# Last part of an attention-and-experts kernel: values of the gates in a PSUM bank, normalising spread over the products, and one copy moved to ScalarE

## The chip, the cores and the metric

The kernel runs on one core of a Trainium2 chip. Its engines are named as in the profile: PE (TensorE, matmuls and transposes), ACT (ScalarE), DVE (VectorE), POOL (GpSimd) and SP (SyncE, which here only issues DMAs). The metric is the device time of one execution in microseconds. Before the change three runs took 1736.75, 1737.0 and 1741.14 us; the median is 1737.0.

## The reference

The input is `x` of shape (4, 32, 128, 128). Two layers follow each other.

```python
# layer 0: each image becomes q of 128 channels x 4096 pixels (2x2 space-to-depth)
energy = einsum('bci,bcj->bij', q, q)          # 4096 x 4096 per image
energy = energy / (d[:, :, None] * d[:, None, :])   # d = sqrt(diagonal)
out = gamma * einsum('bcj,bij->bci', q, softmax(energy)) + xs

# layer 1, on the same values as 4 x 4096 tokens of 128 values
t = t + sum over heads of Q @ (K^T V)           # of _ln_t(t): a linear attention
probs = softmax(_ln_t(t) @ router_w + router_b)  # 8 experts
top_p, top_i = top_k(probs, 2);  top_p /= sum(top_p)
t = t + sum over the two of top_p * (_ln_t(t) @ expert_w[e] + expert_b[e])
```

The second layer has no softmax in its attention, so a product of a 128 x 128 matrix with every token is enough for it. The expert layer adds to each token the output of its two best experts, weighted by their normalised probabilities.

## The kernel before

Per image, the 4096 pixels are cut into 8 chunks of 512. A chunk is loaded, transposed by PE into a bank (`ptq`), copied to SBUF as `qT` (L302), squared and summed (L324, L325), raised to the power -1/2 by POOL (L164), scaled (L338), transposed again and copied as `qn`. This is `prep`; the chunk that everything waits for is the first one of image 0, in two halves (`g` = 0 and 1). Then `attend` walks over pairs of chunks: products of `qn` (L556), exponentials on ACT (L559), value products (L440), and, since the matrix of energies is symmetric, the mirrored share through transposed blocks (L369, L375). That is nearly all of the time, and PE sets it.

The second layer of an image runs while the next image's first layer does, except for the last image, where nothing is left to run beside it. There `last_parts` (L1183 and after) does it with all of the core. Its order is the order of the Python statements: from the end of the prologue on, the program is recorded in an order written out by hand, and each engine keeps it.

The tokens of an image are 32 tiles `k` of 128 tokens. In the last part each goes through these steps:

- The attention's product is added (L1217 to L1220, L1242), then mean and variance are taken (`bn_stats`, `close_stats`). Its power -1/2 is on POOL (L164), followed on POOL by `nbf` and `nbo` (L638, L640).
- `normalise` (L642) writes `xn[:, k]` on ACT, one instruction per tile (L644).
- `transpose_tokens(g)` (L862) turns four tiles by PE into one bank (`ptf`, L870); an ACT copy of 512 columns brings them back to `xn` (L866).
- `router_rows` (L806, lines L811 to L819) makes the eight logits per token on DVE, and `route` (L821, lines L830 to L853) the gates: maximum, exponential (ACT, L832), best and second-best expert, their weights. It is done for 16 tiles at once, so an instruction has 128 x (16 x 8) elements. `route(0)` covers tiles 0 to 15, `route(1)` tiles 16 to 31. The result `gate` is the tile `first`.
- `product(k, h)` (L1197) multiplies tile `k` by four experts (`h` = 0 or 1) into a bank `py` (L1198). Five banks go round for these. `scaled_sums` on DVE (L1141) adds some of the eight experts to `acc`, with `T` or `acc` in SBUF as the other input; `scaled_rows` on ACT (L1155) writes the others, scaled, to `tmp`: 6 of 8 for k below 8, 5 below 14, then 4. POOL adds them up for each two tiles (`sum_rows`, L1163 to L1167), and four DMAs store every four tiles (L1173).

A main loop over k holds the last three. Beside it runs the generator `second_half`, one step per turn: statistics of tiles 16 to 31, `router_rows`, `route(1)`, then normalising and transposing groups 4 to 7. Groups 0 and 1 are ready before the loop; groups 2 and 3 (tiles 8 to 15) are normalised and transposed just ahead of it.

Transposes take their bank from the pool `ps_t` of three, through `psum_t`; `hold` keeps count of banks that are not emptied yet.

Of the kernel before, what the change touches and what calls it, by code (L numbers as in the profile page):

```python
# [15 lines left out]
AF = mybir.ActivationFunctionType  # L16
ALU = mybir.AluOpType
AX = mybir.AxisListType
# [4 lines left out]
def kernel(  # L23
# [74 lines left out]
    def psum_t(name):  # L98
        return ps_t.tile([P, CH], F32, tag="pt", name=name)
# [182 lines left out]
    def prep(b, kc, st):  # L282

        if b == 0:
            if kc == 0:
                st["all"] = big1.tile([P, 4, 8, HW2, 2], F32, tag="T", name="xx_0")
            xx = st["all"][:, kc]
        else:
            xx = xin.tile([P, 8, HW2, 2], F32, tag="xx", name=f"xx_{b}_{kc}")
        first = b == 0 and kc == 0  # L290
        load_tokens(
            xx.rearrange("p k w r -> p k (w r)"), b, 8 * kc, 8, (nc.sync, nc.scalar if first else nc.sync)
        )
        qT = qpool.tile([P, 2, NJ, P], F32, tag="qT", name=f"qT_{b}_{kc}")
        st.setdefault("qT", {})[2 * kc] = qT[:, 0]
        st["qT"][2 * kc + 1] = qT[:, 1]
        yield
        yield
        yield from idle(2 if b else 1)

        def load_half(g, pt):
            nc.vector.tensor_copy(  # L302
                qT[:, :, 2 * g : 2 * g + 2, :].rearrange("p s j (r c) -> p (j r) s c", c=64),
                pt.rearrange("p (m s c) -> p m s c", s=2, c=64),
            )

        for g in range(2):
            yield
            pt, done = hold(f"ptq_{b}_{kc}_{g}", partial(load_half, g))
            for jj in range(2):  # L310
                for r2 in range(2):
                    k = 4 * g + 2 * jj
                    nc.tensor.transpose(
                        pt[:, ts(2 * jj + r2, P)], xx[:, k : k + 2, :, r2].rearrange("p k w -> p (k w)"), ident
                    )
            yield
            done()
        yield
        yield
        ss = stat.tile([P, 2 * NJ], F32, tag="ss", name=f"ss_{b}_{kc}")  # L320
        rn = stat.tile([P, 2 * NJ, 1], F32, tag="rn", name=f"rn_{b}_{kc}")
        for s in range(2):
            sq = work.tile([P, NJ, P], F32, tag="qs", name=f"sq_{b}_{kc}_{s}", bufs=2)
            nc.vector.tensor_tensor(sq, qT[:, s], qT[:, s], ALU.mult)  # L324
            nc.vector.tensor_reduce(ss[:, ts(s, NJ)], sq, AX.X, ALU.add)  # L325
            if first:
                pow_neg_half(rn[:, ts(s, NJ), 0], ss[:, ts(s, NJ)])
            elif s == 1:
                pow_neg_half(rn[:, :, 0], ss)
            yield  # L330
            yield
        yield from idle(1)
        if first:
            keep_running(22, ps_g, "pg")
        scaled = []
        for s in range(2):
            qs = work.tile([P, NJ, P], F32, tag="qs", name=f"qs_{b}_{kc}_{s}", bufs=2)
            nc.vector.tensor_tensor(qs, qT[:, s], rn[:, ts(s, NJ)].to_broadcast([P, NJ, P]), ALU.mult)  # L338
            scaled.append(qs)
        for s, qs in enumerate(scaled):  # L340
            yield
            qn = npool.tile([P, CH], F32, tag="qn", name=f"qn_{b}_{2 * kc + s}")
            st.setdefault("qn", {})[2 * kc + s] = qn
            pt, done = hold(f"ptn_{b}_{kc}_{s}", lambda p, qn=qn: nc.scalar.activation(qn, p, AF.Copy))  # L344
            for j in range(NJ):
                nc.tensor.transpose(pt[:, ts(j, P)], qs[:, j, :], ident)
            yield
            done()
        yield
        yield  # L350
# [251 lines left out]
    def layer1(b, st):  # L602
# [200 lines left out]
                    bank[:, ts(j - j0, D + 2 * E)], keep[k // 4][:, ts(k % 4, P)], matx, start=True, stop=True  # L803
                )

        def router_rows(eng, r0, nr, la):  # L806

            sh = [P, nr, E]
            rows = slice(r0, r0 + nr)
            w1, w2 = (stat.tile([P, 16, E], F32, tag=nm, name=f"{nm}_{b}_{r0}", bufs=1)[:, :nr] for nm in ("lw1", "lw2"))  # L810
            eng.tensor_tensor(w1, nba[:, rows].to_broadcast(sh), srw.to_broadcast(sh), ALU.mult)  # L811
            eng.tensor_tensor(w1, la[:, :, E:], w1, ALU.subtract)
            eng.tensor_tensor(w1, w1, sda[:, rows].to_broadcast(sh), ALU.mult)
            eng.tensor_tensor(w1, w1, la[:, :, :E], ALU.add)
            yield
            eng.tensor_tensor(w2, nbf[:, rows].to_broadcast(sh), srw.to_broadcast(sh), ALU.mult)
            eng.tensor_tensor(w2, w2, rb_sb.to_broadcast(sh), ALU.add)
            eng.tensor_tensor(w1, w1, rsf[:, rows].to_broadcast(sh), ALU.mult)
            eng.tensor_tensor(lg[:, rows], w1, w2, ALU.add)  # L819

        def route(h):  # L821

            sh = [P, KT // 2, E]
            rows = slice(h * KT // 2, (h + 1) * KT // 2)
            ms, dn = (stat.tile([P, KT // 2, 1], F32, tag=nm, name=f"{nm}_{b}_{h}") for nm in ("ms", "dn"))
            pr = stat.tile(sh, F32, tag="prob", name=f"prob_{b}_{h}", bufs=1)
            mx = weight[:, 1, rows]
            o1, o2 = first[:, rows], second[:, rows]
            v = lg[:, rows]
            nc.vector.tensor_reduce(mx, v, AX.X, ALU.max)  # L830
            nc.vector.tensor_tensor(pr, v, mx.to_broadcast(sh), ALU.subtract)
            nc.scalar.activation(pr, pr, AF.Exp)  # L832
            yield
            nc.vector.scalar_tensor_tensor(o1, pr, 1.0, rank.to_broadcast(sh), ALU.is_equal, ALU.mult)
            nc.vector.tensor_reduce(ms, o1, AX.X, ALU.max)
            nc.vector.tensor_tensor(o1, o1, ms.to_broadcast(sh), ALU.is_equal)
            nc.vector.scalar_tensor_tensor(pr, o1, -2.0, pr, ALU.mult, ALU.add)
            yield
            nc.vector.tensor_reduce(mx, pr, AX.X, ALU.max)
            nc.vector.tensor_tensor(o2, pr, mx.to_broadcast(sh), ALU.is_equal)  # L840
            nc.vector.tensor_tensor(o2, o2, rank.to_broadcast(sh), ALU.mult)
            nc.vector.tensor_reduce(ms, o2, AX.X, ALU.max)
            yield
            nc.vector.tensor_tensor(o2, o2, ms.to_broadcast(sh), ALU.is_equal)
            nc.vector.tensor_scalar(dn, mx, 1.0, None, ALU.add)
            nc.vector.reciprocal(dn, dn)
            if not alone:
                nc.vector.tensor_copy(weight[:, 0, rows], dn)
                nc.vector.tensor_tensor(mx, mx, dn, ALU.mult)
                return  # L850
            nc.vector.tensor_tensor(o2, o2, mx.to_broadcast(sh), ALU.mult)
            nc.vector.tensor_tensor(o1, o1, o2, ALU.add)
            nc.vector.tensor_tensor(gate[:, rows], o1, dn.to_broadcast(sh), ALU.mult)  # L853

        def add_rows(u, j0, la, pa):
            nj = min(3, 8 - j0)
# [326 lines left out]
        def last_parts():  # L1183
# [53 lines left out]
            def second_half():  # L1237

                bs, stats = batch_stats("f", 16, 16)
                for u in (2, 3):  # L1240
                    tg = T[:, ts(u, 8), :]
                    nc.vector.tensor_tensor(tg, tg, copies[u], ALU.add)  # L1242
                    yield
                    for j in range(8):
                        stats[8 * u - 16 + j]()
                        if j % 4 == 3:
                            yield
                close_stats("f", 16, 16, bs)
                yield
                logits = router_rows(nc.vector, 16, 16, la[:, 16:])  # L1250
                next(logits)
                yield
                yield
                for _ in logits:
                    pass
                gates = route(1)
                next(gates)
                yield
                for g in range(4, 8):
                    normalise(range(4 * g, 4 * g + 4), rsf, nbo)  # L1260
                    next(gates, None)
                    yield
                    transpose_tokens(g)()
                    yield
# [15 lines left out]
                pass  # L1280
            products = [product(k, h, bank(f"py_{b}_{k}_{h}")) for k in range(2) for h in range(2)]
            transpose_tokens(1)()
            normalise(range(8, 16), rsf, nbo)
            transpose_tokens(2)()
            transpose_tokens(3)()
            for k in range(KT + 4):
                if k < KT:
                    n = by_scalar(k)
# [6 lines left out]
                    sum_rows(k // 2 - 1, by_scalar(k - 2), nc.vector if k == KT else nc.gpsimd)  # L1295
                if k >= 5 and k % 4 == 1:
                    store(k // 4 - 1)
                if k >= 1:
                    next(rest, None)

# [102 lines left out]
```

## Time and profile before

| | us |
|---|---|
| median of the runs (3) | 1737.0 |
| the profiled execution | 1730.18 |
| its span, first to last instruction | 1728.4 |
| PE busy | 1656.8 (96%) |
| DVE busy | 939.3 (54%) |
| ACT busy | 925.8 (54%) |
| POOL busy | 511.8 (30%) |
| DMA, mean over the span | 206 GB/s |

All the rest is from the profiled execution, and its times count from the start of the span. The last part looks like this, by stretches (busy us of each engine):

| stretch | length | PE | DVE | ACT | POOL |
|---|---|---|---|---|---|
| 1652.0 to 1657.0 | 5.00 | 3.54 | 2.53 | 4.57 | 0.00 |
| 1657.0 to 1668.0 | 11.00 | 10.66 | 9.30 | 9.49 | 7.38 |
| 1668.0 to 1681.0 | 13.00 | 9.88 | 11.63 | 7.78 | 12.52 |
| 1681.0 to 1690.4 | 9.40 | 7.00 | 8.88 | 7.95 | 6.52 |
| 1690.4 to 1697.9 | 7.50 | 7.39 | 5.23 | 6.79 | 5.57 |
| 1697.9 to 1720.6 | 22.70 | 22.58 | 17.82 | 16.15 | 18.75 |

Where a row of the timeline merges several instructions, its duration is from the first start to the last end. "[0.16 <-PE ptq L313]" after a row is the idle time of the engine ahead of it and what ended it. [...]

### The profile page before, as it was taken

To read this page: it belongs to the slowest core of one execution; us is meant where nothing else is said; L and a number is where in the kernel's file an instruction comes from. 1 tells how busy PE (TensorE), PEld (TensorE's weight loads), DVE (VectorE), ACT (ScalarE), POOL (GpSimd) and SP (SyncE) were. 2 spreads that over 40 slices of the span, in tenths; PEclk is the share of its full clock that TensorE was granted. 3 is DMA by queue.
4 is the path that set the end of the run, shared out by engine and by line. 5 is a ranking of instruction groups with operands and counts; after the bars stand their busy time and mean duration, and the time that the engine had idled before them with its cause. 6 is when DMAs were issued, how large, how long until landed. Compare 5 with 4: busy or idle time off the path is not lost. (4 is left out here: it accounts for less than half of the span.)

```text
span 1728.4 us, 21211 instructions
## 1 busy us (share of the span) xinstructions
PE 1656.8 (96%) x5458; PEld 876.9 (51%) x5458; DVE 939.3 (54%) x2443; ACT 925.8 (54%) x2893; POOL 511.8 (30%) x553
## 2 busy tenths in 40 slices
PE   7999999999999999989999999999999999999887
PEld 4444444455554456445564455545555445544633
DVE  4433334367485235467568334557748524455686
ACT  3555445465565455446565544546656545545376
POOL 1000000011026514550014631652102650453156
PEclk9999999999999999989999999999999999999999
DMA  4775778876569899996568979998656988995001
GB/s 128 202 206 170 205 208 238 250 213 183 158 195 271 241 259 262 246 257 182 168 189 228 277 230 262 283 252 231 183 163 196 269 242 260 269 259 135 1 13 38
DMA packets 240681, 355.25 MB, mean 206 GB/s; under 512 B 27312, under 2 KB 155312, under 8 KB 226480
## 3 DMA queue, kind: packets, MB, share of 16 engines
q1 hardware_dynamic: 220048, 314.91, 64.5%
q0 software_dynamic: 12288, 25.19, 4.9%
q10 hardware_dynamic: 8224, 13.77, 2.8%
q8 instruction: 46, 0.75, 0.2%
q14 instruction: 75, 0.61, 0.1%
HBM read 183.64 MB, written 173.15 MB: 206 GB/s over the span
## 5 line engine op out<-in xcount | busy, mean ns | idle before, releaser
L559 ACT ACTIVATE pr<-pe 128x512 f32<-128x512 f32 (+1 forms) x576 | 322.4, 560 | 557.0 <-PE pe L556 428.8
L440 PE MATMUL po<-pr,qT 128*128 128x512 f32 (+3 forms) x1152 | 552.9, 562 | 3.9 <-ACT o L445 3.4
L375 PE MATMUL pg<-G,qT 128*128 128x512 f32 x880 | 453.4, 597 | 14.1 <-DMA G<-blocks 8.7
L556 PE MATMUL pe<-qn,qn 128*128 128x512 f32 x896 | 462.5, 598 | 3.3 <-ACT pr L559 3.0
L369 DVE STREAM_TRANSPOSE F<-pr 128x512 f32<-128x512 f32 x440 | 306.1, 702 | 156.1 <-ACT pr L559 132.1
L440 PEld LDWEIGHTS po<-pr,qT 128*128 128x128 f32 x1152 | 216.6, 191 | 251.8 <-issue 224.4
L380 ACT ACTIVATE junk<-G 128x512 bf16<-128x512 f32 x440 | 273.0, 621 | 7.1 <-DMA G<-blocks 7.0
L375 PEld LDWEIGHTS pg<-G,qT 128*128 128x128 f32 x880 | 167.5, 192 | 214.0 <-issue 187.0
L1114 POOL DMA_INDIRECT yb<-ys,place x192 | 185.5, 966 | 262.5 <-DMA xn<-xs 96.3
L989 POOL DMA_INDIRECT xs<-xn,place x192 | 186.1, 969 | 132.2 <-ACT pr L559 55.3
L556 PEld LDWEIGHTS pe<-qn,qn 128*128 128x128 f32 x896 | 155.3, 192 | 115.9 <-issue 103.0
L385 DVE TENSOR_TENSOR o<-o,pg 128x512 f32<-128x512 f32 x110 | 75.5, 686 | 203.1 <-PE pg L375 164.6
L164 POOL TENSOR_TENSOR rn<-ss,neg_half 128x8 f32<-128x8 f32 (+1 forms) x17 | 26.9, 1586 | 334.1 <-DVE ss L325 334.1
L559 ACT ACTIVATION_READ_ACCUMULATOR pr<-pe 128x1 f32 x576 | 112.1, 195 | 0.0
L1023 ACT ACTIVATE xn<-pys 128x256 f32<-128x256 f32 (+1 forms) x120 | 45.0, 377 | 118.3 <-PE pys L1056 67.7
L1049 PEld LDWEIGHTS pys<-ew_sb,xn 128*128 128x128 f32 x468 | 68.5, 192 | 56.3 <-issue 39.0
L164 POOL TENSOR_TENSOR rsf<-dm_f,neg_half 128x8 f32<-128x8 f32 (+1 forms) x15 | 26.2, 1748 | 233.7 <-DVE sv_f L636 233.7
L556 PE MATMUL pe<-qn 128*128 128x512 f32 (+3 forms) x256 | 91.1, 438 | 0.7 <-ACT qn L344 0.7
L164 POOL TENSOR_TENSOR rsa<-dm_a,neg_half 128x8 f32<-128x8 f32 x16 | 26.4, 1650 | 219.3 <-DVE sv_a L636 219.0
L380 ACT ACTIVATION_READ_ACCUMULATOR junk<-G 128x1 f32 x440 | 84.4, 192 | 0.0
L1049 PE MATMUL pys<-ew_sb,xn 128*128 x468 | 72.1, 277 | 11.1 <-ACT xn L1023 11.0
L1032 DVE COPY result<-pys 128x256 f32<-128x256 f32 (+1 forms) x60 | 24.6, 411 | 96.5 <-ACT xn L1023 48.7
(189 smaller groups left out, 1607.6 us busy)
## 6 DMA issues: line engine op xcount, KB each, us to landing
blocks<-F SPq DMA_DIRECT2D x108, 1024.0 KB
G<-blocks SPq DMA_DIRECT2D x432, 256.0 KB
xn<-xs SPq DMA_DIRECT2D x114, 128.0 KB
below<-F SPq DMA_DIRECT2D x31, 384.0 KB
G<-below SPq DMA_DIRECT2D x124, 96.0 KB
out_dram<-acc SPq DMA_DIRECT2D x128, 64.0 KB
xx<-in_x_dram SPq DMA_DIRECT2D x62, 128.0 KB
ys<-xn SPq DMA_DIRECT2D x60, 128.0 KB
```

The source lines that it names most:

```text
L164: pinned(nc.gpsimd.tensor_tensor(dst, src, neg_half.to_broadcast(list(src.shape)), ALU.pow))
L369: f()
L375: nc.tensor.matmul(pg.rearrange("p (a f) -> p a f", a=4), st["qT"][i][:, ib, :], G[:, :, ib], start=(ib == 0), stop=(ib == NJ - 1),)
L380: nc.scalar.activation(junk, G[:, :, ib], AF.Copy, accum_out=st["sums"][:, NJ * i + ib, jc : jc + 1])
L385: nc.vector.tensor_tensor(o, o, pg.rearrange("p (a j c) -> p a j c", a=4, c=S), ALU.add)
L440: nc.tensor.matmul(row["po"][:, lo:hi], qT[blk // NJ][:, blk % NJ, :], w, start=start, stop=(row["left"] == 0))
L556: nc.tensor.matmul(pe[:, c0:], qn[jc][:, ts(j, P)], qn[i][:, c0:], start=True, stop=True)
L559: nc.scalar.activation(pr[:, c0:], pe[:, c0:], AF.Exp, accum_out=sums[:, t, i : i + 1]).ins
L989: inst = nc.gpsimd.indirect_dma_start(xs[h], offset(place[:, i, k : k + 1]), xn[:, k, :], None)
L1023: nc.scalar.activation(bufs[4 + g % 2][:, :n], p[:, : n * P].rearrange("p (j t) -> p j t", t=P), AF.Copy)
L1049: nc.tensor.matmul(p[:, 2 * P + j * D : 2 * P + j * D + D], bufs[4 + g % 2][:, j, :], weights[:, bass.ds(begins[2 * (g % 2) + j], D)], sta ...
L1114: inst = nc.gpsimd.indirect_dma_start(yb[k // 4][:, i, k % 4, :], None, ys, offset(place[:, i, k : k + 1]))
```

## The change

Three edits:

1. In `prep`, the second half (`g` = 1) of the very first chunk is copied from its bank to `qT` by ACT instead of DVE. All other copies stay on DVE.
2. In the last part, `router_rows` and `route` for tiles 16 to 31 get `temps`, four pieces of 128 x (16 x 8) values in one bank of the pool `ps_t`. Intermediate values (`w1`, the first of the second sum, the logits, `ranks`, `pr`, `o2`) are in it instead of SBUF. The shifted logits `w2`, the one-hot matrix `first` and small values per token stay in SBUF. In `route` without `temps` only the tile that takes the last sum differs (`o2` instead of `o1`).
3. The eight normalising instructions for tiles 8 to 15 and the transposes of groups 2 and 3 leave their place ahead of the loop. Turn k of the loop, for k below 8, normalises tile 8 + k, and turns 3 and 7 transpose groups 2 and 3.

```diff
         def load_half(g, pt):
-            nc.vector.tensor_copy(
-                qT[:, :, 2 * g : 2 * g + 2, :].rearrange("p s j (r c) -> p (j r) s c", c=64),
-                pt.rearrange("p (m s c) -> p m s c", s=2, c=64),
-            )
+            dst = qT[:, :, 2 * g : 2 * g + 2, :].rearrange("p s j (r c) -> p (j r) s c", c=64)
+            src = pt.rearrange("p (m s c) -> p m s c", s=2, c=64)
+            if first and g == 1:
+                nc.scalar.activation(dst, src, AF.Copy)
+            else:
+                nc.vector.tensor_copy(dst, src)
...
-        def router_rows(eng, r0, nr, la):
+        def router_rows(eng, r0, nr, la, temps=None):
...
+            w0, sums = w2, lg[:, rows]
+            if temps is not None:
+                w1, w0, sums = temps[:, 0], temps[:, 1], temps[:, 0]
...
-            eng.tensor_tensor(w2, nbf[:, rows].to_broadcast(sh), srw.to_broadcast(sh), ALU.mult)
-            eng.tensor_tensor(w2, w2, rb_sb.to_broadcast(sh), ALU.add)
+            eng.tensor_tensor(w0, nbf[:, rows].to_broadcast(sh), srw.to_broadcast(sh), ALU.mult)
+            eng.tensor_tensor(w2, w0, rb_sb.to_broadcast(sh), ALU.add)
             eng.tensor_tensor(w1, w1, rsf[:, rows].to_broadcast(sh), ALU.mult)
-            eng.tensor_tensor(lg[:, rows], w1, w2, ALU.add)
-
-        def route(h):
+            eng.tensor_tensor(sums, w1, w2, ALU.add)
+
+        def route(h, temps=None):
...
             v = lg[:, rows]
+            ranks = o1
+            if temps is not None:
+                v, ranks, pr, o2 = (temps[:, n] for n in range(4))
...
-            nc.vector.scalar_tensor_tensor(o1, pr, 1.0, rank.to_broadcast(sh), ALU.is_equal, ALU.mult)
-            nc.vector.tensor_reduce(ms, o1, AX.X, ALU.max)
-            nc.vector.tensor_tensor(o1, o1, ms.to_broadcast(sh), ALU.is_equal)
+            nc.vector.scalar_tensor_tensor(ranks, pr, 1.0, rank.to_broadcast(sh), ALU.is_equal, ALU.mult)
+            nc.vector.tensor_reduce(ms, ranks, AX.X, ALU.max)
+            nc.vector.tensor_tensor(o1, ranks, ms.to_broadcast(sh), ALU.is_equal)
...
-            nc.vector.tensor_tensor(o1, o1, o2, ALU.add)
-            nc.vector.tensor_tensor(gate[:, rows], o1, dn.to_broadcast(sh), ALU.mult)
+            nc.vector.tensor_tensor(o2, o1, o2, ALU.add)
+            nc.vector.tensor_tensor(gate[:, rows], o2, dn.to_broadcast(sh), ALU.mult)
...
-                logits = router_rows(nc.vector, 16, 16, la[:, 16:])
+
+                temps = psum_t("gates").rearrange("p (n k e) -> p n k e", n=4, e=E)
+                logits = router_rows(nc.vector, 16, 16, la[:, 16:], temps)
...
-                gates = route(1)
+                gates = route(1, temps)
...
             transpose_tokens(1)()
-            normalise(range(8, 16), rsf, nbo)
-            transpose_tokens(2)()
-            transpose_tokens(3)()
...
                 if k >= 5 and k % 4 == 1:
                     store(k // 4 - 1)
+                if k < 8:
+                    normalise(range(8 + k, 9 + k), rsf, nbo)
+                    if k % 4 == 3:
+                        transpose_tokens(2 + k // 4)()
                 if k >= 1:
                     next(rest, None)
```

## The prediction

> **What bounds the kernel now.** I read the page first: PE is busy 1656.8 us of a span of 1728.4 (96%), so a change far from PE's queue is worth nothing in the long middle. The diff, however, touches only the first microseconds and the last 80, where the slices of PE fall to 8, 8 and 7 tenths. So I went on to the chain of waits from 1652 us. Start, duration, engine, result and line, a few pieces of it:
>
> ```profile
> 1653.03 3.07 ACT xn L644 x8
> 1656.10 1.02 ACT xn L866 x2
> 1657.69 5.61 PE py L1198 x12
> ...
> 1668.60 2.94 POOL rsf L164
> ...
> 1672.48 1.83 DVE lw L818
> ...
> 1676.87 1.55 DVE first L834
> ...
> 1690.42 2.81 PE py L1198 x6
> ...
> 1697.94 2.41 PE py L1198 x5
> ```
>
> Three stretches are to be seen. Up to 1657.1 ScalarE (ACT) normalises eight token tiles and copies two transposed groups while the products wait. From 1663.3 to 1690.3 the chain runs through DVE (and once POOL): that is routing of the second half. From 1690.4 on it is PE with few holes.
>
> The timeline of DVE and POOL says why DVE is slow there (start, duration, engine, line, operation, shape):
>
> ```profile
> 1672.25 1.90 POOL L1163 TENSOR_TENSOR tmp<-tmp 128x768 f32<-128x768 f32 x1
> 1672.40 1.90 DVE L818 TENSOR_TENSOR lw<-lw,rsf 128x128 f32<-128x128 f32 x1
> ...
> 1676.44 1.81 POOL L1163 TENSOR_TENSOR tmp<-tmp 128x768 f32<-128x768 f32 x1
> 1676.78 1.62 DVE L834 SCALAR_TENSOR_TENSOR first<-prob,rank 128x128 f32<-128x128 f32 x1
> ```
>
> The same L818 took 0.28 and the same L834 0.27 for the first half, with POOL idle. Here each ends just as POOL's instruction ends. L1141, which reads a product from a bank, is not hurt: all 106 lie between 339 and 353 ns, whatever POOL does.
>
> For the start, the timeline:
>
> ```profile
> 7.06 0.69 DVE L302 COPY qT<-ptq 128x512 f32<-128x512 f32 x1 [7.06 <-PE ptq L313]
> 7.91 0.69 DVE L302 COPY qT<-ptq 128x512 f32<-128x512 f32 x1 [0.16 <-PE ptq L313]
> 8.64 1.29 DVE L324 TENSOR_TENSOR sq<-qT 128x512 f32<-128x512 f32 x2
> 13.20 0.60 ACT L344 ACTIVATE qn<-ptn 128x512 f32<-128x512 f32 x1 [8.76 <-PE ptn L346]
> ```
>
> The second copy is directly ahead of the squares, and ACT does nothing until 13.20.
>
> [...]the trace has 0.351 for L1141 against 0.286 for equal SBUF work. [...]No row of this case has DVE writing a bank.
>
> **The change, part by part.** The order of instructions on all five queues is otherwise the old one; no wait is added to the later transposes, though the gates hold one of three banks.
>
> *Start.* One DVE copy (0.69) goes, one ACT copy comes. Nearest row: ACT L344, the same size from a bank, 0.60. 7.91 + 0.60 = 8.51, and some 0.08 to hand over: squares at 8.59 in place of 8.64. Gain 0.05; bounds: 0.1 gained, 0.2 lost if the four-step output pattern or the hand-over is slow. ACT's idle 8.76 us hides the rest.
>
> *Gates in a bank.* The 24 routing instructions of the second half sum to 13.4 us on the timeline, those of the first half to 6.7. Of the excess of 6.7, the single-input L845 (0.69 against 0.17) keeps 0.5, and 0.065 for each of some 20 instructions costs 1.3. DVE gets about 5 us back. A write into the bank is unknown: from nothing to as much again (1.3); I take nothing. `exp` in place on ACT (0.31) stays as it is.
>
> *Normalising spread.* Out of the head go 3.07 + 1.02 = 4.1 us of ACT; the same eight rows (0.39 each by start to start) and two copies (0.50) come back inside products 0 to 7. ACT's sum does not change; its first scaled row starts after the first two L1141 (1652.58 to 1653.3), not at 1657.02: 3.7 earlier. What is late next?
>
> *DVE and POOL.* Products 0 and 1 leave ACT at 1656.9, not 1660.2, so POOL's first sums begin 3.3 earlier, its power (L164) too, and the routing's second part (L816) starts at about 1668.7 instead of 1671.86. From there 6 routing instructions at 0.38 (2.3), three L1141 (1.0), the exp behind ACT's product 8 (to 1672.7), 4 + 4 + 6 routing instructions (4.9), and the sums of products 10 to 14 (5.7) end at about 1683.2. Before, 1690.3: 7.1 earlier.
>
> *ACT*, in its queue order, from 1653.35: products 0 to 3 with a normalised row each, 4 x (1.57 + 0.39) = 7.8; then the transposed group waits for its last row, 0.5 (first group: normalising ends 1645.50, copy 1645.91), and its copy 0.5; the same for 4 to 7: 1671.0. Product 8, exp, product 9: 1.27 + 0.3 + 1.27; four rows 1.54: 1675.4. Product 10 to the start of the next copy 2.08 (1681.09 to 1683.17 now, PE's transposes between), copy 0.5: 1678.0. Product 11 1.25, rows 1.54, product 12 with its copy 2.6: 1683.4. Product 13 and rows 2.8: 1686.2. Product 14 takes 1.0, and the copy of group 6 starts at about 1687.4. Now: 1693.71. So ACT gives 6.3, DVE has 1.5 us to spare, and ACT is last.
>
> *PE* has from 1652.4 to that copy 30 products at 0.86 and five groups at 0.6, 28.8 us of 35; it waits, but never 2.7 us at a time as it does before 1677.38, after which two products took 3.41 instead of 1.72. The waits that I find are under 1 us.
>
> Behind the copy of group 6 nothing changes: 1728.4 - 1693.7 = 34.7 us; POOL's sums (2.8 us for two products against PE's 3.44) keep up.
>
> *Sum.* 1687.4 + 34.7 = 1722.1, a gain of 6.3. Walking PE, ACT, DVE and POOL forward together, each instruction at the later of its queue and its inputs, I get 6.0; the same walk over the queues as they are ends within 0.2 of the trace. I take **6.0 us**: a span of 1722.4. The profiled execution took 1730.18 (1.8 outside the span), so 1724.2 there; the median of the runs, 1737.0, lies 6.8 above that execution, and I carry the difference over: **1731.0 us**.
>
> **Rivals.** *Only the bank pays* (-3.4, 1733.6): ACT's waits for the transposes inside the loop eat what the early start gave. For it: ACT is last in my sum. Against: it needs 2.6 us more waiting in four places that I priced from rows. *Only the spread pays* (-1.8, 1735.2): instructions on the bank stay blocked by POOL, DVE stays last, and the gain is the earlier start of POOL less DVE's new collisions with it. Against: L1141's even 0.351. *The change doesn't do it*: the held bank delays a later group of transposes. The built queues have no such wait, so this is nearly out.
>
> *Slower*: DVE instructions that write the bank are dear. 18 of them lie between L816 and product 14; DVE has 1.5 us to spare, so at x more each the gain is gone when 18x = 6.0 + 1.5, x = 0.42, an instruction of 0.77 instead of 0.35. At 1.05 us each the kernel is 5.4 us slower: 1742.4. Against: the size is 128 elements, and no reading of a bank shows such a price.
>
> **How the numbers follow.** 0.3% of 1737.0 is 5.2 us, about what a measurement can tell from no change. Both parts as summed: 0.66, with its own range 1729.5 to 1732.8 (writes dearer by 0.065, waits 1 us either way). One part alone: 0.25 (bank 0.15, spread 0.10). Slower: 0.09, of which 0.07 beyond 5.2 us. My 6.0 lies close to 5.2: of 0.66 I count 0.57 beyond it, and 0.02 of the partial cases; faster 0.59, same 0.34, slower 0.07. The range, with 2 us of spread between runs: 1728.0 to 1735.5; it leaves out the slower case and the upper end of the partial one.
>
> **What would show it.** Second-half routing instructions near 0.3 to 0.36 us beside POOL's; the first scaled row near 1653.4; L816 near 1668.7; the copy of group 6 near 1687.4; PE without a hole above 1 us from 1652 to 1720; squares at 8.6. I am wrong if routing instructions still end with POOL's, if the bank's take 0.7, or if ACT waits on the transposes for more than 3 us in sum.

## The result and the profile after

The changed kernel takes 1728.79 us (median of seven runs, 1722.72 to 1730.52); the kernel before, run beside it, 1736.75 us (seven runs, 1729.58 to 1741.14). The ratio is 0.9952, with a 95% interval of 0.9929 to 0.9975: faster by 8 us, between 4.3 and 12.3. On another chip, in the experiments below, the changed kernel gave 0.9967 (0.9948 to 0.9986). The forecast was 1731.0.

The profiled execution of the changed kernel happens to be the longest of its seven: 1730.52 us, span 1728.7. It reaches the last part 6.8 us later than that of before, for reasons ahead of it, so its clock times can't be laid beside the old ones. A common point can: the **first sum**, the first row by L1149 (L1141 in the kernel before), at 1659.41 after and at 1652.58 before. Times with a plus sign below count from it. What lies ahead of it on DVE doesn't change: in every profile of this study ScalarE's copy of the transposed group 0 starts 6.64 to 6.67 us before the first sum.

The start, timeline of the changed kernel (start, duration, engine, line, operation, shape, and the idle time ahead with what ended it):

```profile
7.86 0.60 ACT L305 ACTIVATE qT<-ptq 128x512 f32<-128x512 f32 x1 [3.43 <-PE ptq L315]
8.49 1.29 DVE L326 TENSOR_TENSOR sq<-qT 128x512 f32<-128x512 f32 x2 [0.79 <-ACT qT L305]
```

The transposes of the second half end at 7.83 and the squares start 0.66 later. Before it was 7.88 and 0.76.

Routing beside POOL, timeline of the changed kernel, some rows of POOL's sums (L1171 and L1175, formerly L1163 and L1167) and the routing rows L823, L842 and L844, which answer to L818, L834 and L836 of before:

```profile
1675.76 1.80 POOL L1171 TENSOR_TENSOR tmp<-tmp 128x768 f32<-128x768 f32 x1
1676.04 0.30 DVE L823 TENSOR_TENSOR gates<-gates,rsf 128x128 f32<-128x128 f32 x1
...
1679.13 0.72 POOL L1175 TENSOR_TENSOR acc<-acc,tmp 128x256 f32<-128x256 f32 x1
1679.27 0.30 DVE L842 SCALAR_TENSOR_TENSOR gates<-gates,rank 128x128 f32<-128x128 f32 x1 [0.92 <-ACT gates L840]
...
1679.82 1.81 POOL L1171 TENSOR_TENSOR tmp<-tmp 128x768 f32<-128x768 f32 x1
1679.93 0.29 DVE L844 TENSOR_TENSOR first<-gates,ms 128x128 f32<-128x128 f32 x1
```

The three DVE rows lie wholly inside a POOL row and take 0.29 to 0.30 us, where the first two took 1.90 and 1.62. L844 has one input in the bank and one in SBUF and writes to SBUF, so a result in SBUF does not hold it up either. The 24 routing rows of the second half sum to 7.19 us (13.43 before).

The chain of waits of the changed kernel, some pieces from the first sum on:

```profile
1660.18 0.64 ACT tmp L1163 x2
1660.86 6.92 PE py L1206 x14
...
1668.44 0.60 ACT xn L874
...
1680.55 1.10 ACT xn L646 x3
...
1684.04 0.60 ACT xn L874
...
1685.93 1.52 ACT xn L646 x4
...
1691.31 1.52 ACT xn L646 x4
```

No DVE routing piece is left in it behind the first sum. It is mostly TensorE (PE) up to 1677 and, from there to 1694, mostly ScalarE (ACT). What those two wait for between 1659 and 1698, from the table of waits (microseconds in all, times, the longest):

```profile
ACT xn L874 <- PE ptf L878: 2.2, 4, 0.7
ACT tmp L1163 <- DVE acc L1149: 2.0, 1, 2.0
PE py L1206 <- ACT tmp L1163: 3.9, 4, 2.5
```

ScalarE's wait of 2.0 us is that for the first sum itself; the four for transposed groups (0.42, 0.42, 0.68, 0.68) are the only ones after it. TensorE's longest wait, 2.5 us, is also at the first sum (0.75 in a second profile of the changed kernel).

| from the first sum to | before | after |
|---|---|---|
| first scaled row on ACT | +4.44 | +0.77 |
| second part of the routing (L816, now L821) | +19.28 | +15.97 |
| last routing row ends | +36.27 | +28.28 |
| copy of group 6 on ACT | +41.13 | +34.41 |
| last addition on DVE ends | +70.85 | +64.13 |

The last part is 6.7 us shorter between these two profiles. From the copy of group 6 to the last addition it is 29.72 us in both.

### The profile page after: what moved, and what is told of

Same layout as the page of the kernel before. It is cut to its first block, busy times and chain, and to the rows that moved or that the text cites. A ratio compares the mean times of both kernels' runs of the same rounds, so it can differ in the third digit from the quotient of the medians.

```text
span 1728.7 us, 21209 instructions
## 1 busy us (share of the span) xinstructions
PE 1658.9 (96%) x5458; PEld 877.3 (51%) x5458; DVE 932.4 (54%) x2442; ACT 926.6 (54%) x2894; POOL 511.9 (30%) x553
## 5 line engine op out<-in xcount | busy, mean ns | idle before, releaser
L164 POOL TENSOR_TENSOR rsa<-dm_a,neg_half 128x8 f32<-128x8 f32 x16 | 26.5, 1659 | 218.6 <-DVE sv_a L638 218.2
```

The costliest lines, as they stand in the source:

```text
L164: pinned(nc.gpsimd.tensor_tensor(dst, src, neg_half.to_broadcast(list(src.shape)), ALU.pow))
```

## The experiments

All the ratios are to the kernel before on the same chip, and the last part is measured from the first sum to the end of the last addition. It repeats well: two profiles of the changed kernel give 64.13 and 64.10, two of edit 2 alone 65.13 and 65.14. That makes a profile the sharper measure, since single runs of one kernel differ by 10 us and more. The kernel before repeats less well, and that is taken up with the clock, further down.

| kernel | ratio (95%) | first scaled row | copy of group 6 | last addition | 24 routing rows, sum |
|---|---|---|---|---|---|
| before, three profiles | 1 | +4.44, +4.46, +2.89 | +41.13, +42.47, +40.84 | +70.85, +72.17, +70.56 | 13.43, 13.79, 13.03 |
| edit 2 alone (bank) | 0.9967 (0.9956 to 0.9979) | +2.75 | +35.42 | +65.13 | 6.97 |
| edit 3 alone (spread) | 0.9978 (0.9966 to 0.9991) | +0.77 | +37.84 | +67.54 | 13.42 |
| whole change, pieces in SBUF | 0.9988 (0.9973 to 1.0002) | +0.77 | +37.76 | +67.48 | 13.04 |
| whole change | 0.9967 (0.9948 to 0.9986) | +0.76 | +34.39 | +64.10 | 7.19 |
| whole change, 18 more copies | 0.9956 (0.9942 to 0.9970) | +0.77 | +34.95 | +64.67 | 12.31 with the copies |
| whole change, copies later | 0.9930 (0.9909 to 0.9951) | +0.77 | +32.77 | +61.69 | 7.28 |

The second profile of the kernel before in this table is that of edit 1 alone, whose last part is the old one.

### Each edit alone

Edit 2 alone is the change's `temps` in `router_rows` and `route`, with the start and the normalising of before:

```diff
-                logits = router_rows(nc.vector, 16, 16, la[:, 16:])
+                temps = psum_t("gates").rearrange("p (n k e) -> p n k e", n=4, e=E)
+                logits = router_rows(nc.vector, 16, 16, la[:, 16:], temps)
...
-                gates = route(1)
+                gates = route(1, temps)
```

> Edit 2 alone: the kernel before, with the second half's gates in a bank; start and normalising as before. My theory (both parts pay, and each leaves the other's limit standing): routing instructions of the second half at 0.28 to 0.30 us beside POOL, but products 0 and 1 leave ScalarE as late as before; 3.4 us less than before, ratio about 0.998. From the first L1141 to the copy of group 6: 41.1 us before, 34.4 with the whole change, about 37.7 here. Rival, the bank is the whole gain: ratio 0.995 and about 34.5 us for that stretch. Rival, the bank is worth nothing and the spread is all: ratio 1.000 and 41 us.

Measured: 0.9967, and +35.42 to the copy of group 6, where 37.7 was expected. Routing is at 0.29 to 0.30 us. The bank alone brings 5.4 us of the last part (70.56 to 65.13, both without a low clock ahead of the first sum), of which an estimated 1.3 is a long low clock in that profile of the kernel before (see the part on the clock); the other 4.1 is still more than my theory's 3.4. "The spread is all" is out. "The bank is the whole gain" is out by the profiles alone (65.13 against 64.13 and 64.10): the ratios of edit 2 and of the whole change overlap.

Edit 3 alone:

```diff
-            normalise(range(8, 16), rsf, nbo)
-            transpose_tokens(2)()
-            transpose_tokens(3)()
...
+                if k < 8:
+                    normalise(range(8 + k, 9 + k), rsf, nbo)
+                    if k % 4 == 3:
+                        transpose_tokens(2 + k // 4)()
```

> Edit 3 alone: the kernel before, with tiles 8 to 15 normalised and transposed inside the loop; gates stay in SBUF. My theory: first scaled row 0.8 us behind the first sum instead of 4.4, but second-half routing instructions again end with POOL's instructions (1.6 to 1.9 us where they meet), DVE is last; 1.8 us less than before by the prediction, up to 3.5 if fewer of them meet POOL at the new times; ratio 0.998 to 0.999, and 37.6 to 39.3 us from the first sum to the copy of group 6. Rival, the spread is the whole gain: ratio 0.995 and 34.5 us.

Measured: 0.9978, +37.84 to the copy of group 6, 67.54 in all. That is 3.3 us less than the first profile of before and 4.6 less than the second, both with the same low clock ahead of the first sum as here, and 3.0 less than the third, without it. L818 is at 1.91 us and L834 at 1.62, as before, and all 24 rows sum to 13.42 against 13.43: the same collisions, 3.3 us earlier. So each edit pays alone. Against the same profile of before (70.56) they bring 5.4 and 3.0 us, and together 6.4 to 6.5, less than the sum. Both shorten the way to the same event, ScalarE's copy of group 6, and both take away the same long low clock, which can go only once; how much either counts for is not shown.

Edit 1 alone is the change's `load_half` in the kernel before:

```diff
+            if first and g == 1:
+                nc.scalar.activation(dst, src, AF.Copy)
+            else:
+                nc.vector.tensor_copy(dst, src)
```

> Edit 1 alone: the kernel before, with the second half of the very first rows copied by ScalarE. Theory: ScalarE's copy 0.60 us and a hand-over of 0.03 to 0.08, so the squares start 0.63 to 0.68 us behind the end of the transposes instead of 0.77, a gain of about 0.1 us that a time of 1737 us can't show. Rival: the hand-over or the output in four steps makes it as long as DVE's copy, no gain. The last part is that of the kernel before: 70.85 us from the first sum to the last addition if TensorE's clock dips while it makes products 0 and 1, as in the first profile, and 69.2 if it does not.

Measured: the copy takes 0.60 us, the squares start 0.66 us behind the end of the transposes; in another profile of the kernel before it is 0.76. The gain is 0.10 us. The last part, with a low clock ahead of the first sum, took 72.17 us and not 70.85; the part on the clock returns to it.

### Is it the place or the separate pieces?

The change also writes fewer results over their inputs. This kernel has every instruction of the changed one in the same order and with the same inputs, but the four pieces lie in SBUF:

```diff
-                temps = psum_t("gates").rearrange("p (n k e) -> p n k e", n=4, e=E)
+                temps = work.tile([P, CH], F32, tag="grp", name=f"gates_{b}", bufs=2).rearrange("p (n k e) -> p n k e", n=4, e=E)
```

> The whole change, but the four pieces for the gates lie in SBUF (a buffer of 128 x 512 that is free in the last part); every instruction, its order and its inputs are those of the changed kernel. Theory, it is the place of the inputs: instructions with two inputs in SBUF end with POOL's again, single-input reductions stay at 0.28, and the time is that of the spread alone, 1.8 to 3.5 us less than before (ratio 0.998 to 0.999). Rival, it is the separate pieces (fewer results written over their inputs): routing instructions at 0.3 us and ratio 0.995, as the changed kernel.

Timeline of DVE in this kernel:

```profile
1661.84 1.90 DVE L823 TENSOR_TENSOR gates<-gates,rsf 128x128 f32<-128x128 f32 x1
...
1666.22 1.61 DVE L842 SCALAR_TENSOR_TENSOR gates<-gates,rank 128x128 f32<-128x128 f32 x1
1667.87 0.29 DVE L843 TENSOR_REDUCE ms<-gates 128x16 f32<-128x128 f32 x1
```

And of POOL at the same time:

```profile
1661.68 1.90 POOL L1171 TENSOR_TENSOR tmp<-tmp 128x768 f32<-128x768 f32 x1
...
1665.88 1.81 POOL L1171 TENSOR_TENSOR tmp<-tmp 128x768 f32<-128x768 f32 x1
```

L823 and L842 end with POOL's instruction again (POOL at 1663.58 and 1667.69, DVE at 1663.74 and 1667.83). The reduction L843 has one input and takes 0.29 us, although POOL's next instruction runs from 1667.77 on. The last part is 67.48 us, that of the spread alone. So it is the place, and the separate pieces bring nothing.

The other side of it is the kernel before, with gates in SBUF, without POOL's sums for tiles 0 to 13. This leaves out a part of the experts' result, so its time counts for nothing.

```diff
-                if 1 <= k <= KT and k % 2 == 0:
+                if 14 < k <= KT and k % 2 == 0:
```

> The kernel before without POOL's sums of the scaled rows for tiles 0 to 13 (that part of the experts' result is left out); gates stay in SBUF. Theory, POOL's instructions are what the routing instructions of the second half wait for: L816 to L853 at 0.28 to 0.30 us, their 24 in all near 6.7 us, as in the first half. Rival, it is something else that runs only there (ScalarE writing, TensorE's products, the stores): they stay at 0.5 to 1.9 us.

Timeline of DVE:

```profile
1661.19 0.28 DVE L818 TENSOR_TENSOR lw<-lw,rsf 128x128 f32<-128x128 f32 x1
...
1663.39 0.28 DVE L834 SCALAR_TENSOR_TENSOR first<-prob,rank 128x128 f32<-128x128 f32 x1
```

All rows of 128 elements are at 0.23 to 0.29 us, and the 24 sum to 6.69 (L845 and L846, which are smaller, take 0.17 and 0.25). With POOL quiet, two inputs in SBUF cost nothing extra here.

### Who is last: ScalarE or DVE?

To put a price on dearer work with the bank, 18 copies out of it were added behind the routing rows of the second half (`again(x)` is a DVE copy of `x` to an SBUF tile `spare`):

```diff
             eng.tensor_tensor(w0, nbf[:, rows].to_broadcast(sh), srw.to_broadcast(sh), ALU.mult)
+            again(w1)
...
             nc.vector.tensor_reduce(mx, v, AX.X, ALU.max)
+            again(v)
```

> The changed kernel, with a copy of 128 values per partition (one piece of the bank to an SBUF tile that nobody reads) behind each of the 18 routing instructions of 128 elements from L821 on: about 0.3 us of DVE more for each, 5.4 to 5.9 us in all, which stands for a dearer write into the bank. Theory, ScalarE sets the stretch and DVE has 1.5 us to spare by the prediction: the last part is 4 us longer than the changed kernel's 64.1 us (from the first sum to the last addition). Rival, DVE has none to spare: 5.4 to 5.9 longer. Rival, its idle time in the stretch (1.1 and 0.85 us before the sums of products 14 and later, 0.9 at the exponential) takes nearly all of it: 2.5 us or less longer.

Timeline of DVE, two of the pairs:

```profile
1657.18 0.28 DVE L846 TENSOR_REDUCE weight<-gates 128x16 f32<-128x128 f32 x1
1657.38 0.28 DVE L847 COPY spare<-gates 128x128 f32<-128x128 f32 x1
1657.57 0.29 DVE L848 TENSOR_TENSOR gates<-gates,weight 128x128 f32<-128x128 f32 x1
1657.90 0.29 DVE L849 COPY spare<-gates 128x128 f32<-128x128 f32 x1
```

The routing rows now sum to 12.31 us, 5.1 more, but rows overlap: L847 starts 0.20 us behind L846 and L848 0.19 behind L847, though each is listed with 0.28 or 0.29. From first start to last end, the four batches of routing rows behind L821 became 3.8 us longer (6.3 to 10.2 in all), so the load was smaller than the 5.4 to 5.9 meant. The last part grew by 0.54 to 0.57 us, to 64.67. With 1.5 us to spare, 3.8 would have cost 2.3, and with nothing to spare 3.8: my theory and the first rival fall also at this load. DVE absorbed about 3.3 us that it had to spare; the second rival is right.

If ScalarE is last, its waits for transposed groups are on the path. In this kernel each such copy comes one product later, behind the scaled rows of the next tile:

```diff
-                        transpose_tokens(2 + k // 4)()
+                        late.append(transpose_tokens(2 + k // 4))
...
                     scaled_rows(k, products[:2], n)
+                    while late:
+                        late.pop()()
...
-                    transpose_tokens(g)()
+                    late.append(transpose_tokens(g))
```

> The changed kernel, with each ScalarE copy of a transposed group (groups 2 to 7) placed behind the next product's scaled rows instead of at once behind its transposes; nothing else moves. Theory, ScalarE sets the stretch up to the copy of group 6: its waits for transposes there (0.42, 0.42, 0.68, 0.68 us) go, and the kernel is about 2 us faster than the changed one (8.0 + 2 us less than before, ratio about 0.994). Rival, DVE or TensorE is already as late: no more than 0.5 us, ratio 0.995.

Timeline of ScalarE in it, the copies of groups 2 and 4 (a row's duration runs to its end, the next one starts up to 0.35 us earlier):

```profile
1646.61 0.81 ACT L874 ACTIVATE xn<-ptf 128x512 f32<-128x512 f32 x1
...
1661.02 0.69 ACT L874 ACTIVATE xn<-ptf 128x512 f32<-128x512 f32 x1
```

No idle time is left ahead of them. The last part is 61.69 us, 2.4 less than with the change, and the ratio 0.9930. (The copy of group 6 itself now stands one product later in ScalarE's queue, so that its +32.77 is not the same point as the +34.39 of the change; the scaled rows of product 14 start at +30.77 instead of +33.29.) Since its interval touches that of the change, both were run once more on one chip:

> The changed kernel once more, beside the next one on the same chip. Ratio 0.995 to 0.996; 64.1 us from the first sum to the last addition.

> The changed kernel with the copies of transposed groups one product later, once more, beside the changed kernel on the same chip. If the first run of it is right: 2.4 us less than the changed kernel in the last part (61.7 us from the first sum to the last addition), ratio 0.993 to 0.9945. Rival, the first run's lower time was chance: ratio as the changed kernel's.

Measured: the changed kernel 0.9967 (median 1712.21), the one with later copies 0.9939 (0.9918 to 0.9960; median 1707.39), and 64.10 against 61.67 us in the last part. The version with later copies beats both kernels; it leads the changed one by 2.4 us in both profiles, and by 4.8 in these medians. Its gain is about as large as the four waits (2.2). Together with the little that a load on DVE costs, it shows that ScalarE, and not DVE, is last on the way to the copy of group 6.

### TensorE's clock

The granted clock goes with the differences between the profiles of the kernel before. Busy time by stretches in its first profile (stretch, length, busy us and rows of PE, PE's weight loads, DVE, ACT, POOL, then the granted clock, DMA's share and GB/s):

```profile
1646.50:1652.00 5.50, 5.44 (x10) 2.37 (x11) 5.05 (x22) 1.74 (x6) 0.00 (x0) 0.69 0.00 0
1677.40:1681.00 3.60, 3.39 (x4) 0.90 (x4) 3.43 (x8) 2.48 (x8) 3.44 (x5) 0.55 0.00 0
```

The clock falls to 0.50 twice, for 3.41 us each: at products 0 and 1 (5.40 us for eight rows instead of 3.70), and behind TensorE's idle time of 2.68 us, at the products that took 3.41 us for four rows. Below, the first is the early fall, from about 5.5 us ahead of the first sum, and the other the second fall, from +24.5 or later. More profiles were to show what they cost:

> The kernel before once more, for one question: its first profile shows products 0 and 1 at a granted clock of 0.69 (5.40 us for eight rows instead of 3.70). Theory: this dip comes in some executions and not in others, and costs the kernel before 1.6 to 1.7 us there, since ScalarE starts its eight normalising instructions behind the transposes that follow: 69.2 us from the first sum to the last addition without the dip, 70.85 with it. Rival: ScalarE's start makes no difference there, since DVE is last: 70.8 us either way.

> Edit 2 alone once more, for the same question. Its first profile had no dip in products 0 and 1, and 65.1 us from the first sum to the last addition. Theory: with the dip 66.8, without it 65.1. Rival: 65.1 either way.

The kernel before once more:

```profile
1636.00:1641.40 5.40, 4.33 (x13) 2.08 (x13) 4.95 (x21) 2.90 (x8) 0.00 (x0) 1.00 0.00 0
1666.00:1673.00 7.00, 5.71 (x11) 2.22 (x10) 6.11 (x17) 3.76 (x12) 5.59 (x8) 0.54 0.16 37
```

This time the clock fell only at +0.64, behind products 0 and 1, and the first scaled row came at +2.89 instead of +4.44; but the second fall was 6.83 us long. The last part took 70.56. The profile of edit 1 alone had both, the early fall and the long second one: 72.17. So the early fall costs the kernel before 1.6 us (72.17 against 70.56), and 3.41 us more of the second one cost it 1.3 (72.17 against 70.85), each by one pair of profiles. The short second fall costs nothing: in the first profile the chain of waits is DVE's from +19.3 to +37.8, and in the two with the long one products of TensorE stand in it (+28.9 and +31.9 in that of edit 1 alone). My expectation for this run (69.2) did not allow for the second. The changed kernel has no second fall in either profile, and the early one costs it nothing (64.10 with it, 64.13 without): its ScalarE waits for DVE's first sum anyway. Edit 2 alone had no early fall in the second profile either, so the 66.8 that I gave for it were not put to the test.

So what the change is worth depends on the clock of the execution that it is compared with. With the early fall in the profile of before it is 6.7 us (edit 3 alone 3.3). Without it, and with a short second fall, the kernel before would take an estimated 69.2 (70.85 less 1.6), and the gains would be 5.1 for the whole, 4.1 for edit 2 alone and, if the early fall costs edit 3 as little as the whole change, 1.7 for edit 3 alone.

Does the idle time bring the second fall? The kernel before, with 20 idle transposes in the gap:

```diff
+                            if (k + 2, h) == (11, 0):
+                                keep_running(20)
```

> The kernel before, with 20 transposes that nobody reads between the two halves of product 11, where TensorE stands idle for 2.4 to 2.7 us in three profiles of it; in each of the three the granted clock falls to 0.50 about 1 us after that idle time ends and stays there for 3.3 to 7 us. Theory, the idle time brings the fall, and the fall costs the last part 1.3 us or more: no clock below 1.00 between 20 and 40 us behind the first sum, the first to the last addition 1.3 to 3 us shorter than in a profile of the kernel before with the same clock ahead of the first sum (70.85 and 72.17 with the early fall, 70.56 without). Rival, DVE is last there and TensorE's clock is hidden: no fall, but the same 70.6 to 72.2. Rival, the clock falls in any case: low clock between 24 and 32 us as before.

```profile
1677.00:1684.00 7.00, 5.17 (x26) 2.84 (x25) 6.65 (x15) 3.33 (x11) 6.73 (x8) 1.00 0.00 0
1684.00:1689.00 5.00, 4.68 (x10) 2.44 (x11) 4.02 (x12) 3.70 (x13) 3.46 (x5) 0.66 0.23 52
```

The gap was filled, and the fall came all the same, at +28 instead of +24 or +25, behind a gap of 1.97 us that follows, and for 3.41 us. The last part is 69.81, 0.75 less than in the profile with the same early clock, where 1.3 to 3 was expected; the ratio is 0.9987 (0.9972 to 1.0001). So the run moved the idle time instead of taking it away, and it can't tell my theory from the rival that the clock falls in any case. The filler was transposes; whether products in the gap would have kept the clock up was not tried.

The 14 profiles together say more. In each, every fall starts a whole number of steps of 3.41 us from the others (to 0.003 us) and lasts one step or two, the one at the very end apart. Where these steps lie against the kernel's work differs from execution to execution. I cut the traces into these steps, from 1600 us ahead of the first sum to 58 us behind it, and took those at full clock:

| TensorE busy in the step | steps | followed by a step at 0.50 |
|---|---|---|
| below 41% | 86 | 86 |
| 41 to 45% | 18 | 10 |
| above 45% | 6572 | 12 |

In each of the 12, TensorE did mostly transposes (9 of 10 rows in the one that the first profile of before has, from 8.9 us ahead of the first sum on). The step ahead of the second fall is busy to 21%, 21% and 40% in the three profiles of the kernel before, and to 42% with the gap filled. Edit 3 alone has a gap of 2.0 us in that place too, but its step is at 47% (53% with the pieces in SBUF), and no fall follows. Nor does one follow the changed kernel's wait of 2.46 us at the first sum, which lies across two steps (49% and 79%). So in these profiles the second fall goes with the idle time, where enough of it lies within one step. This is read from traces as they came; no run set the gap against the steps on purpose, and why some falls last two steps is open.

## Why the prediction was right, point by point

- **Start.** 0.05 was forecast, with 0.1 as the upper bound; it is 0.10. The hand-over takes 0.03 us, where I had taken 0.08.
- **Gates in a bank.** That an instruction with an input in the bank does not end with POOL's was my estimate, from L1141's 0.339 to 0.353 us beside POOL. It held (0.28 to 0.30 us beside POOL), and the runs with the pieces in SBUF (13.04 us for the 24 rows) and without POOL's sums (6.69) bear it out. The price was wrong: 0.065 for each of 20 instructions was charged for reading the bank. They take 0.28 to 0.30 us, within 0.03 of what they take from SBUF with POOL quiet (L859 apart, 0.05 more). The sum fell by 6.2 us instead of 5. The unknown price of writing a bank, taken as nothing, is nothing that can be seen. L853 with its single input still meets POOL (0.48 against 0.17, where 0.69 was feared; it ends at 1686.56, POOL's L1172 at 1686.53). The 0.351 and 0.286 that the price is the difference of belong to two kinds of instruction: L1083 of the kernel before, the same multiplication and addition as L1141 with its tensor in SBUF, has a median of 0.351 us over 192 rows.
- **Normalising spread.** First scaled row 3.7 earlier was forecast and is 3.67; but the profile behind the forecast had the early fall, and against the one without it the row comes only 2.1 earlier (2.89 to 0.77). The routing's second part 3.2 was and is 3.3.
- **DVE and POOL.** The sums of product 14 end 8.0 us earlier (28.28 and three L1149 behind it) instead of 7.1, since a bank price of 1.3 us was not due. That part of this came back as waiting, for the exponential and for products, is likely and was not measured apart.
- **ACT last.** 6.3 earlier at the copy of group 6 was forecast (its steps add up to 1687.2, which is 6.5 earlier) and is 6.7. The waits for transposes were charged as 0.5 each and are 0.42 and 0.68. Behind the copy nothing changed, as said. Up to 1677 it is TensorE that stands in the chain, which the walk of ACT alone did not have.
- **DVE's 1.5 us to spare** is the step that failed. It was stated from the walk without its working, and the two gains beside it (7.1 for DVE, 6.3 for ACT) differ by 0.8. The 18 copies show about 3.3, and DVE's idle time (1.1 and 0.85 us ahead of the sums of products 15 and 16, 0.9 at the exponential) is where they can have found room. The slower rival's break-even of 0.42 us each was therefore set too low: 3.8 us more in 18 places, 0.21 each, should have cost 2.3 us and cost 0.6.
- **TensorE without a hole above 1 us** is wrong at one place: 2.46 us at the first sum. Products 0 and 1 ran at full clock in that execution and were done early; in the other profile, with the early fall, the hole is 0.75 us and the last part the same. The idle time and the slow products of before are gone, as forecast, but the products were slow by the clock (0.50), which the prediction did not see.
- **Rivals.** "Only the bank" was put at 3.4 us, and edit 2 alone brings 5.4 (4.1 less the long second fall). It lacks 1.0 us against the whole (35.42 against 34.41 at the copy of group 6), where the prediction had 2.6; with the early fall it might lack more, and no profile of it has that. It starts its scaled rows 2 us later, but has no waits for the transposes of groups 2 and 3 inside the loop, 0.84 us of the difference. "Only the spread" was put at 1.8 and is 3.0 to 4.6: the new collisions that I charged don't come, the 24 rows keep their sum to 0.01 us. "The change doesn't do it" is out: the held bank delays no group, the waits of groups 4 and 5 for their transposes are 0.68 before and after. "Slower" is out with the price of the bank; its 5.4 us at 1.05 us each comes to 5.1 by its own terms.
- **Sum.** 6.0 forecast; 6.7 in the last part by the two first profiles, 6.4 to 8.0 over the three profiles of before; 8.0 in the medians on one chip and 5.6 on another. That it came so close is in part luck. The profile that the sum starts from happened to have the early fall and a short second one (without the early one the estimate is 5.1), and the wrong price of the bank did little harm because it fell on DVE, which was not last. The median of before moved from 1737.0 to 1736.75 when it was run again. Of the 2.2 us between 1731.0 and 1728.79, some 0.7 is seen in the last part, 0.05 at the start and 0.25 in that median; the rest is not explained and lies within the interval of 4.3 to 12.3.

## What to carry to other kernels

When a DVE instruction's end coincides with a POOL instruction's end, count its SBUF inputs. Moving one input to a bank took 13.4 us of routing to 7.2 here, and the same instructions with the same layout in SBUF stayed at 13.0. Before pricing what is left, ask which engine is last by loading another one (3.8 us of copies on DVE cost 0.6 us) and by taking waits off the suspect (four waits of ScalarE gave 2.4 us). When the effect is no larger than the spread of the runs, measure the changed stretch from a landmark in its own profile, and look at the granted clock there first: it moved the kernel before by up to 1.6 us.

## What the runs showed of the hardware that was not expected

- Reading and writing a bank cost the DVE routing instructions of 128 elements almost nothing against SBUF: 0.27 to 0.30 us for all of the 22 such rows, with one input, two inputs, reductions and in place, some 0.2 us more in all than for the first half in SBUF (one of them, L859, takes 0.27 instead of 0.23). L1149, which also reads a bank, stays at 0.33 to 0.35, and L1083 with its tensor in SBUF has the same median, 0.35.
- DVE rows of 0.28 to 0.29 us started 0.19 to 0.20 us apart in places, so the sum of their durations overstated the load: the 18 copies sum to 5.1 us and made the batches 3.8 us longer.
- TensorE's granted clock fell to 0.50 in steps of 3.41 us, one or two at a time; 12 of 14 profiles have such a fall between 6 us ahead of the first sum and 6 us behind it, and the kernel before has a second one. At half clock two products (four rows) took 3.41 us. All 86 steps at full clock in which TensorE was busy for less than 41% were followed by one at 0.50.
